# Decoder layer on one core: looks placed between the exponentials of the first attention, its norms moved ahead, and one of three context forms of each batch made in the own stage

## The chip, the cores and the metric
The kernel runs on one core of a Trainium2 chip. The metric is device time in microseconds (us) of one execution, from the first to the last instruction of the program with what lies around it; less is better. Before the change the median of three runs is 1250.8 us (1247.96 to 1253.37).

The core has five engines that run side by side, each through its own queue in order: PE (TensorE, the matmuls; PEld are its weight loads), DVE (VectorE), ACT (ScalarE), POOL (GpSimd) and SP (SyncE, which issues the DMAs). [...]

## What is computed
One decoder layer over x of 8 batches x 112 tokens x 512, in float32, with a context of 8 x 375 x 512:

```python
x = x + attn(layernorm(x))            # 16 heads of 32, rotary, causal, softmax
x = x + xattn(layernorm(x), context)  # see below
x = x + ffn(layernorm(x))             # ternary weights, silu(gate) * up, rms_norm, projection
```

The second line holds two attentions beside each other. The normed x is divided by an input scale, clipped and rounded to an 8-bit float. From it come q, k and v of the *own* attention (16 query heads and 8 key heads of 128, over the batch's own 112 tokens) and the query of the *context* attention, whose keys and values are projections of the context in full precision. Queries and keys are layer-normed per head. Both outputs are divided by a smoothing vector, rounded to 8 bits again, and go through one projection.

## The kernel before, in words
The order of the work is written out by hand: every engine runs its instructions in the order in which the Python code issues them. There is no planner that moves them. The work falls into four parts.

**First attention** (L417 to L745, about 0 to 168 us). The batches are treated in two halves of four (HB = 4).
- `norm_stats` and `ln_apply` norm a batch on DVE, with two small POOL steps between; `transposed(half)` turns the four normed batches on PE, and ACT copies them into hT.
- `project_qk(half, oc)` makes one of eight 128-row blocks of q and k for four batches: eight matmuls (L494), a bias copy qb on ACT (L502), a shuffle and a product on DVE (L506, L514), a product and a sum on POOL (L513, L515). qb and sw have two buffers each.
- `batch(b, last)` is software-pipelined over batches: `values(b)`, `attended(b - 2)`, `scores(b)`, `turned(b - 1)`, `softmaxed(b)`. In the first half `softmaxed` adds the mask and takes maxima on DVE (L570, L575), subtracts on POOL (L577) and takes exponentials on ACT (L580), for four banks r. `turned` transposes p on PE (L589) and copies it on ACT (L593). `attended` multiplies by v (L605), and DVE divides (L615, L616) into o, which has two buffers.
- `joined(b, ...)` adds o of batch b to x on POOL (L682), takes the statistics of batch b - 1 and norms batch b - 2 into h.
- `quantise_turn` transposes h (L347), `quantise_begin` scales it and takes magnitudes on ACT (L365, L215), and `quantise(n, ...)` clips on DVE (L219, L220) and finishes on POOL (L222, L391). They prepare the 8-bit input of the next part.
- `look(n)` reads through the projection weights of the cross attention once, in 32 pieces: each look is one ACT pass (L462) over a 128 x 512 piece of wp with a sum, to learn whether any low half of a weight is other than zero. A wp tile of 1 MB holds four looks, there are two buffers, and the fourth look of a tile issues the load of the tile after next. Thirteen looks stand among the first projections, four behind each of the first four batches, three among the second projections.

**Own stages** (units 0 to 31: four stages s of eight batches b, about 168 to 440 us). Each unit projects q, k and v of four heads, norms, scores, weighs and attends, with its later steps delayed by one to five units (`advance`). At the end of each unit stand the splitting of weights for later (`own_background`) and `form_parts`.

**Context stages** (units 32 to 63, four stages of eight batches, about 440 to 1057 us). A context batch is used in three pieces j of 125 positions, each in three float32 *forms* (rounded, mixed, rest; 750 KB in all). A form is made from 250 KB of raw context by an ACT copy, a POOL subtraction and a DVE mix, and stored to HBM by SP; later stages load it (`load_ct`). `keys(j)` multiplies piece j by the weights (L1013), ACT and DVE join the two banks (L1023, L1024), DVE takes statistics. Before the change `form_parts` makes the three forms of batch 0 in the own stage (begun in units 10, 14 and 18; the mix in the next unit, L1173; the store in the unit after that), and in the first context stage (s = 4) each unit b from 0 to 6 makes all three forms of batch b + 1 beside its own work with `make_begin` (ACT L1411, POOL L1412) and `make_end` (DVE L1418, store L1422). The tiles come from a pool of four. `made` and `ahead` (L261, L262) say which forms are made where; `queue` is the order in which SP loads raw weights and raw context through five buffers.

**Feed-forward** (about 1057 to 1249 us), with the ternary weights prepared earlier in pieces (`background`).

Of the kernel before, what the change touches and what calls it, by code (L numbers as in the profile page):

```python
# [20 lines left out]
B, S, H = 8, 112, 512  # L21
HB = B // 2
# [3 lines left out]
SC, NJ, CJ = 375, 3, 125  # L26
# [13 lines left out]
def decoder_layer(  # L40
# [39 lines left out]
    def uid(s):  # L80
        count[0] += 1
        return f"{s}_{count[0]}"
# [175 lines left out]
    queue = [(0, what, k) for what in (0, 1) for k in range(KC)]  # L258


    made = {b: [("form", b + 1, j) for j in range(NJ)] for b in range(B - 1)}  # L261
    ahead = [(0, j) for j in range(NJ)]  # L262
    for s in range(8):
        if s == 4:

# [110 lines left out]
    def quantise(n, begin=True):  # L376


        for _ in range(n):
            if begin:  # L380
                quantise_begin()
            t = qstate["clipped"]
            if t < qstate["begun"] - (2 if begin else 0):
                qstate["t", t] = round_a(*qstate.pop(("y", t)), s0, 4)
                qstate["clipped"] += 1
            t = qstate["done"]
            left = qstate["clipped"] - t
            if left > (1 if begin else 2) or (left and not begin and qstate["clipped"] == qstate["begun"]):
                _, half, k, m = qtiles[t]
                engine = nc.vector if half else nc.gpsimd  # L390
                engine.tensor_tensor(  # L391
                    xq[m][:, k, half * SH : (half + 1) * SH], *qstate.pop(("t", t)), ALU.subtract
                )
                qstate["done"] += 1
# [20 lines left out]
    with ExitStack() as st:  # L415
# [39 lines left out]
        def look(n):  # L455
            for _ in range(n):
                i, k = divmod(looks[0], KC)
                looks[0] += 1
                w = looked[i][:, k * 512 : (k + 1) * 512].bitcast(U16).rearrange("p (n two) -> p n two", two=2)
                half = w[:, :, 0:1].rearrange("p n o -> p (n o)")  # L460
                at = KC * i + k
                nc.scalar.activation(half, half, AF.Copy, accum_out=seen[:, at : at + 1])  # L462
                if k == KC - 1:
                    look_load()
# [97 lines left out]

        def softmaxed(banks, masked):

            ps_ = []
            for r in range(4):
                p = a2.tile([S, 4, S], F32, tag="p", name=uid("p"), bufs=8)
                s_ = banks[r][:S, :SH].rearrange("p (h t) -> p h t", t=S)
                if not masked:
                    nc.vector.tensor_tensor(  # L570
                        p, s_, mask.rearrange("p (o t) -> p o t", o=1).to_broadcast([S, 4, S]), ALU.add
                    )
                    s_ = p
                nm = sm("amx", 4)
                nc.vector.tensor_reduce(nm[:S], s_, AX.X, ALU.max, negate=True)  # L575
                engine = nc.vector if masked else nc.gpsimd
                engine.tensor_tensor(  # L577
                    p, s_, nm[:S].rearrange("p (h o) -> p h o", o=1).to_broadcast([S, 4, S]), ALU.add
                )
                nc.scalar.activation(p, p, AF.Exp)  # L580
                ps_.append(p)
            return ps_
# [82 lines left out]
        for i, oc in enumerate((0, 4, 1, 5, 2, 6, 3, 7)):  # L665
            project_qk(0, oc)
            if i > 2:
                look(2 if i < 5 else 3)
            if i == 1:
                for b in range(HB, B):  # L670
                    lns[b] = norm_stats(xb[b])
            elif i == 2:
                for b in range(HB, B):
                    ln_apply(b)
            elif i == 3:
                transposed(1)
        va, pr, pt = {}, {}, {}

        def joined(b, least, last):

            if b < last:
                nc.gpsimd.tensor_tensor(xb[b], xb[b], outs.pop(b), ALU.add)  # L682
            if least <= b - 1 < last:
                stats_x[b - 1] = norm_stats(xb[b - 1], True)
            if least <= b - 2 < last:
                h = s0.tile([S, H], F32, tag="h", name=uid("h"), bufs=4)
                norm_apply(h, xb[b - 2], *stats_x.pop(b - 2))
                normed_x[b - 2] = h
# [21 lines left out]

        for b in range(HB):
            batch(b, HB)
            look(4)
        for i, oc in enumerate((0, 4, 1, 5, 2, 6, 3, 7)):
            if i == HB + 3:
                quantise(3, False)
            project_qk(1, oc)
            if i < 3:
                look(1)
            if i < 2:  # L720
                batch(HB + i, HB)
            if i < HB + 2:
                joined(i, 0, HB)
            if i == HB + 2:
                for _ in range(3):
                    quantise_begin()
        first.close()
        for b in range(HB, B):
            batch(b, B, 3 if b < B - 1 else 0)
# [246 lines left out]
    class Context(Unit):  # L976
# [10 lines left out]
        def project(self, g):  # L987
            tile_ = self.b < NT
            if not self.makes:
                load_ct(g + 1, 0)  # L990
            if tile_:
                xqx = xqxs.pop(g)
                project_q(self, lambda k: xqx[:, k, :])
            advance("normed", g)
            advance("weigh", g)
            if tile_:
                qn = self.qn = Heads("cq", P, 4)
                qn.stats(*[self.pq[:, j * P : (j + 1) * P] for j in range(4)])
                qn.powers([(4, epsc[:, 3:4])])
            kn = self.kn = Heads("ckv", CJ, 6)  # L1000
            self.kv = []
            rounds = self.s == 4 and self.b + 2 < NT
            if rounds:
                round_q3(self.b + 2, 0)
            if self.makes:
                make_begin(g + 1, 0)

            def keys(j):
                ct, banks = cts.pop((g, j)), [pa(), pa()]
                for m, bank in ((0, 0), (1, 1), (2, 1)):  # L1010
                    for k in range(KC):
                        at = (m * KC + k) * CJ
                        nc.tensor.matmul(  # L1013
                            banks[bank][:CJ, :],
                            lhsT=ct[:, at : at + CJ] if ct.dtype == F32R else ct[:, at : at + CJ].bitcast(F32R),
                            rhs=split[self.s, 1, k][m],
                            start=(k == 0 and m == bank),
                            stop=(k == KC - 1 and m != 1),
                        )
                if j < NJ - 1 and not self.makes:  # L1020
                    load_ct(g + 1, j + 1)
                kv = c2.tile([CJ, 512], F32, tag="kv", name=uid("kv"), bufs=8)
                nc.scalar.activation(kv, banks[0][:CJ, :], AF.Copy, scale=1.0 - E12)  # L1023
                nc.vector.tensor_tensor(kv, kv, banks[1][:CJ, :], ALU.add)  # L1024
                self.kv.append(kv)
                kn.stats(*[kv[:, i * P : (i + 1) * P] for i in range(2)])

            keys(0)
            if self.makes:
                make_end(g + 1, 0)  # L1030
                make_begin(g + 1, 1)
            advance("out", g)
            background(2 * g)
            advance("turn_p", g)
            if rounds:
                round_q3(self.b + 2, 1)
            keys(1)
            if self.makes:
                make_end(g + 1, 1)
                make_begin(g + 1, 2)  # L1040
            if tile_:
                self.q = c2.tile([P, 512], F32, tag="q", name=uid("q"))
                for j in range(4):
                    qn.normalise(self.q[:, j * P : (j + 1) * P], self.pq[:, j * P : (j + 1) * P], j)
            background(2 * g + 1)
            context_splits(self.s, self.b)
            advance("attend", g)
            advance("turn", g)
            advance("rounded", g)
            split_end()  # L1050
            if rounds:
                round_q3(self.b + 2, 2)
            keys(2)
            if self.makes:
                make_end(g + 1, 2)
            if self.b == NT:
                drop(self.s, 1)
                if self.s < 7:
                    split_chunk(self.s + 1, 0, KC - 1)
            expand_q(g + 1)  # L1060
            kn.powers([(6, LN_EPS)])
            advance("score", g)
# [117 lines left out]
        nc.sync.dma_start(out=forms[b][:, j, :], in_=f.rearrange("p f c -> p (f c)").bitcast(F32))  # L1180


    fparts = {B + 2 + 4 * i: [i] for i in range(len(ahead))}

    def form_parts(i):

# [516 lines left out]
```

## Time and profile before

| | |
|---|---|
| Median of three runs | 1250.8 us |
| Profiled execution, its own time | 1251.02 us |
| Its span, first to last instruction | 1249.2 us |
| Mean granted clock of PE | 0.967 |
| PE, DVE, ACT, POOL busy | 94%, 72%, 67%, 64% of the span |
| Data moved by DMA | 151.37 MB, mean 121 GB/s |

The profile tells of one execution. A busy PE is not PE at its peak, since the ends of pipelined matmuls are modelled; so a stretch is judged by PE's idle time, by who ended it, and by the granted clock, which falls to half at times. Lines of the timeline give the start and the duration in us, the engine, the line of the kernel, the operation, what it writes and reads, its shape and how many follow each other; in brackets stands how long the engine had been idle and whose work ended that. A line of the view by stretches gives the stretch, its length, the busy time of PE, PEld, DVE, ACT and POOL with the number of instructions, the granted clock, the DMA engines' busy share and GB/s.

### The profile page before, as it was taken

How to read it: one execution, taken by the hardware profiler on the slowest of the kernel's cores; microseconds unless marked ns; L12 is line 12 of the kernel's file. 1: busy time of each engine (PE TensorE's matmuls, PEld its weight loads, DVE VectorE, ACT ScalarE, POOL GpSimd, SP SyncE). 2: the span in 40 equal slices, each digit the busy share in tenths (PEclk: the TensorE clock that was granted, in tenths of full speed). 3: DMA queues.
4: the chain of work that ended last, by engine and by line, in shares of the span. 5: the costliest groups of instructions: out<-in, count | busy, mean ns of one | idle time of the engine just before them, and what ended most of it. 6: DMA issues, size and time to landing. Idle time of an engine off the chain costs nothing. (4 is left out here: it accounts for less than half of the span.)

```text
span 1249.2 us, 19832 instructions
## 1 busy us (share of the span) xinstructions
PE 1178.3 (94%) x6312; PEld 932.0 (75%) x6312; DVE 903.2 (72%) x2365; ACT 843.1 (67%) x2083; POOL 805.3 (64%) x962
## 2 busy tenths in 40 slices
PE   8998987899999889999999999999999999999998
PEld 5474776787878767777777777787777877788886
DVE  6557877778887767786777768677776767577764
ACT  2752765978787856767667776677677676466643
POOL 5638746676767756876566676577574666476554
PEclk9988966999999998999999999999999999999999
DMA  7320130222221255456655455554554541122311
GB/s 243 135 68 0 53 118 1 75 87 83 69 85 40 74 178 170 160 179 219 191 160 173 153 176 171 178 162 159 185 159 149 183 155 36 43 90 68 106 51 60
DMA packets 55370, 151.37 MB, mean 121 GB/s; under 512 B 6384, under 2 KB 15728, under 8 KB 54240
## 3 DMA queue, kind: packets, MB, share of 16 engines
q1 hardware_dynamic: 55264, 150.07, 36.9%
q8 instruction: 52, 0.85, 0.3%
q14 instruction: 54, 0.44, 0.1%
HBM read 121.65 MB, written 26.56 MB: 119 GB/s over the span
## 5 line engine op out<-in xcount | busy, mean ns | idle before, releaser
L1013 PE MATMUL pa<-wx,ct 128*125 128x512 f32 x1152 | 294.9, 405 | 0.0
L1013 PEld LDWEIGHTS pa<-wx,ct 128*125 128x125 f32 x1152 | 213.3, 190 | 49.8
L222 POOL TENSOR_TENSOR f8t<-y,big 128x512 f32<-128x512 bf16 (+1 forms) x80 | 98.2, 1230 | 134.6 <-DVE big L220 134.5
L827 POOL TENSOR_TENSOR p<-p,ri 112x500 f32<-112x500 f32 (+1 forms) x128 | 128.5, 1025 | 36.5 <-DVE ri L822 35.2
L1024 DVE TENSOR_TENSOR kv<-kv,pa 125x512 f32<-125x512 f32 x96 | 65.8, 686 | 90.7 <-PE pa L1013 42.0
L1105 ACT ACTIVATE p<-ps,cmx 112x375 f32<-112x375 f32 x128 | 71.7, 573 | 83.6 <-DVE cmx L1104 83.6
L765 PE MATMUL pa<-hi,xq 128*128 128x512 f32 (+2 forms) x352 | 114.9, 351 | 1.6 <-DVE xq L391 1.1
L765 PE MATMUL pa<-lo,xq 128*128 128x512 f32 (+2 forms) x352 | 110.0, 337 | 0.9 <-DVE lo L326 0.9
L1381 PE MATMUL pa<-h3T,wf 128*128 128x512 f32 (+1 forms) x512 | 107.3, 368 | 0.5 <-ACT h3T L1354 0.2
L1381 PEld LDWEIGHTS pa<-h3T,wf 128*128 128x128 f32 x512 | 92.7, 188 | 12.3 <-DVE h3T L1355 1.0
L186 DVE BATCH_NORM_AGGREGATE mv<-bst 128x2 f32<-128x6 f32 (+1 forms) x472 | 86.0, 182 | 16.4
L816 ACT ACTIVATE qT<-ps,hln 128x448 f32<-128x448 f32 (+6 forms) x112 | 57.3, 565 | 47.0 <-PE ps L811 46.7
L1096 PE MATMUL ps<-kT,qT 128*112 128x375 f32 x256 | 86.2, 479 | 0.5 <-ACT kT L1082 0.5
L1272 POOL TENSOR_TENSOR th<-th,tw 128x512 bf16<-128x512 bf16 x48 | 57.3, 1194 | 45.2 <-DVE th L1264 33.4
L185 DVE BATCH_NORM_STATS2 bst<-pa 128x6 f32<-128x128 f32 x280 | 76.1, 272 | 13.9 <-PE pa L765 13.6
L205 ACT ACTIVATE kv<-kv,ckvnm,ckvr 125x128 f32<-125x128 f32 x192 | 77.4, 491 | 5.9 <-POOL ckvnm L201 5.8
L785 PE MATMUL ps<-hi,cq 128*128 128x512 f32 x224 | 78.7, 433 | 0.9 <-ACT p L1105 0.6
L1129 PE MATMUL ps<-pT,kv 125*128 125x224 f32 x384 | 78.0, 353 | 0.0
L765 PEld LDWEIGHTS pa<-hi,xq 128*128 128x128 f32 (+1 forms) x352 | 69.8, 198 | 6.9 <-DVE xq L391 1.8
L765 PEld LDWEIGHTS pa<-lo,xq 128*128 128x128 f32 (+1 forms) x352 | 70.0, 199 | 6.6 <-DVE lo L326 2.2
L1129 PEld LDWEIGHTS ps<-pT,kv 125*128 125x128 f32 x384 | 72.7, 190 | 1.9 <-ACT pT L1122 0.2
L847 POOL TENSOR_TENSOR cq<-f8t,big 128x512 fp32r<-128x512 f32 x56 | 66.0, 1179 | 4.4
(201 smaller groups left out, 3013.4 us busy)
## 6 DMA issues: line engine op xcount, KB each, us to landing
ct<-forms SPq DMA_DIRECT2D x75, 750.0 KB, 4.4
w<-in_wattn SPq DMA_DIRECT2D x96, 256.0 KB, 3.3
forms<-ct SPq DMA_DIRECT2D x21, 750.0 KB, 3.8
wp<-in_wattn SPq DMA_DIRECT2D x8, 1024.0 KB, 4.8
tr<-in_wgu SPq DMA_DIRECT2D x32, 256.0 KB, 4.5
done<-th SPq DMA_DIRECT2D x48, 128.0 KB, 4.3
wh<-done SPq DMA_DIRECT2D x24, 256.0 KB, 3.7
w<-in_ctxT SPq DMA_DIRECT2D x21, 250.0 KB, 3.5
```

Of the source, the lines that this page charges most:

```text
L185: nc.vector.bn_stats(st[: self.rows], a)
L186: nc.vector.bn_aggr(self.mv[: self.rows, self.at, :], st[: self.rows])
L205: nc.scalar.activation(dst, src, AF.Identity, bias=self.nm[:rows, i : i + 1], scale=self.r[:rows, i : i + 1])
L222: nc.gpsimd.tensor_tensor(t, y16, big, ALU.add)
L765: nc.tensor.matmul(out_, lhsT=lhsT, rhs=part[:, cut], start=first and i == 0, stop=last and i == 1)
L785: nc.tensor.matmul(po, lhsT=u.cq[:, j * P : (j + 1) * P], rhs=split[u.s, 2, j][i], **kw)
L827: nc.gpsimd.tensor_tensor(p, p, bc, ALU.mult)
L1013: nc.tensor.matmul(banks[bank][:CJ, :], lhsT=ct[:, at : at + CJ] if ct.dtype == F32R else ct[:, at : at + CJ].bitcast(F32R), rhs=split[sel ...
L1096: nc.tensor.matmul(pp[:S, :SC], lhsT=qT[:, j, :], rhs=self.kT[:, j // 2, :], start=True, stop=True,)
L1105: nc.scalar.activation(self.p[:, j, :], pp[:S, :SC], AF.Exp, bias=nm[:S], accum_out=self.sums[:S, j : j + 1])
L1129: nc.tensor.matmul(po[:, cut], lhsT=self.kv[j][:, 256 + g * P : 256 + (g + 1) * P], rhs=self.pT[:, j, cut], start=(j == 0), stop=(j == NJ ...
L1381: nc.tensor.matmul(pp[:, :n], lhsT=wcur[k][:, m * 256 + blk * P : m * 256 + (blk + 1) * P], rhs=hT[half, k][i], start=(k == 0 and i == 0), ...
```

## The change
- In the first half's `softmaxed` one look stands ahead of each of the four exponentials. The four looks behind each batch are gone, and the three among the second projections stand at i = 2, 3 and 4 instead of 0, 1 and 2. There are 32 looks as before.
- The statistics and norms of batches 4 to 7 stand behind the first and second projection instead of the second and third.
- `joined` of batches 0 and 1 stands behind batches 2 and 3 of the first half, and that of the next four behind the first four of the second projections. The first three `quantise_begin` stand one projection earlier (i = 5 instead of 6), and `quantise(3, False)` stands behind the last projection instead of ahead of it.
- Of each batch from 1 to 7 the third form (j = 2) is made in the own stage. `ahead` has ten forms instead of three, begun in every second unit from 10 to 28. In the first context stage a unit makes two forms and loads the third with `load_ct` after `keys(1)`; the queue of raw loads has seven entries fewer.

```diff
-    made = {b: [("form", b + 1, j) for j in range(NJ)] for b in range(B - 1)}
-    ahead = [(0, j) for j in range(NJ)]
+    made = {b: [("form", b + 1, j) for j in range(NJ - 1)] for b in range(B - 1)}
+    ahead = [(0, j) for j in range(NJ)] + [(b, NJ - 1) for b in range(1, B)]
...
+                if not masked:
+                    look(1)
                 nc.scalar.activation(p, p, AF.Exp)
...
             project_qk(0, oc)
             if i > 2:
                 look(2 if i < 5 else 3)
-            if i == 1:
+            if i == 0:
                 for b in range(HB, B):
                     lns[b] = norm_stats(xb[b])
-            elif i == 2:
+            elif i == 1:
                 for b in range(HB, B):
                     ln_apply(b)
...
         for b in range(HB):
             batch(b, HB)
-            look(4)
+            if b >= 2:
+                joined(b - 2, 0, HB)
         for i, oc in enumerate((0, 4, 1, 5, 2, 6, 3, 7)):
-            if i == HB + 3:
-                quantise(3, False)
             project_qk(1, oc)
-            if i < 3:
-                look(1)
             if i < 2:
                 batch(HB + i, HB)
-            if i < HB + 2:
-                joined(i, 0, HB)
-            if i == HB + 2:
+            if 2 <= i < 5:
+                look(1)
+            if i < HB:
+                joined(i + 2, 0, HB)
+            if i == HB + 1:
                 for _ in range(3):
                     quantise_begin()
+        quantise(3, False)
...
-                if j < NJ - 1 and not self.makes:
+                if j < NJ - 1 and not (self.makes and j < NJ - 2):
                     load_ct(g + 1, j + 1)
...
             keys(1)
             if self.makes:
                 make_end(g + 1, 1)
-                make_begin(g + 1, 2)
...
             keys(2)
-            if self.makes:
-                make_end(g + 1, 2)
...
-    fparts = {B + 2 + 4 * i: [i] for i in range(len(ahead))}
+    fparts = {B + 2 + 2 * i: [i] for i in range(len(ahead))}
```

## The prediction
> **What bounds the kernel now.** The first view is the page's busy shares: TensorE is busy 94% of a span of 1249.2 us, the next engine 72%. The chain that ended last names only the last matmuls (7%), so it does not say which earlier stretch decides. So I cut the span into stages by their first matmuls and asked for busy time by stage. Three rows (stretch, its length, then busy us of PE, PEld, DVE, ACT, POOL; granted clock; DMA share; GB/s):
> ```profile
> 83.75:126.04 42.29, 36.52 (x148) 20.52 (x147) 25.75 (x51) 13.38 (x27) 33.12 (x33) 0.85 0.00 1
> ...
> 440.50:601.80 161.30, 150.97 (x706) 116.84 (x704) 120.92 (x308) 108.55 (x259) 109.46 (x124) 0.96 0.53 178
> 601.80:754.20 152.40, 150.18 (x743) 118.00 (x743) 111.36 (x311) 110.52 (x262) 101.03 (x126) 1.00 0.53 169
> ```
> Row 1 is the second run of first-attention projections: PE stands still for 5.8 of 42.3 us, at a clock of 0.85. Rows 2 and 3 are the first context stage, which makes its forms, and the second, which loads them: 161.3 against 152.4 us, so making them costs at most 8.9 us. In the row of the own stage (252.4 to 375.6, not copied here) PE is busy 116.0 of 123.2 us, DVE and ACT 84%, the clock is 1.00 and the DMA share 0.24.
>
> Then the timeline of PE alone, for its waits in the first attention (start, us, operation; in brackets the idle time ahead and who ended it):
> ```profile
> 26.39 1.59 PE L481 MATMUL ps<-ident,h 112*128 112x112 f32 x12 [1.05 <-DVE h L173]
> 29.18 0.60 PE L481 MATMUL ps<-ident,h 112*128 112x112 f32 x4 [1.20 <-DVE h L173]
> ...
> 56.41 3.69 PE L521 MATMUL ps<-w,hT 128*112 128x512 f32 x8 [2.66 <-ACT pt L593]
> ...
> 111.07 0.32 PE L347 MATMUL ps<-ident,h 112*128 112x112 f32 x1 [1.25 <-DVE h L173]
> 114.61 0.45 PE L347 MATMUL ps<-ident,h 112*128 112x112 f32 x1 [3.22 <-DVE h L173]
> 114.85 5.83 PE L494 MATMUL pa<-hT,w 128*128 128x448 f32 x8
> ```
> The reader is to see that each wait is on a norm (h) or on a copy of ACT (pt), and that the last projection takes 5.83 us where the others take 3.05 (40 matmuls in 15.28 us from 94.35). A further wait of 1.31 on pt stands at 85.54, and the clock in the stretch from 113.4 to 120.1 is 0.50.
>
> **Part 1, first attention: -12.0 us.**
> (a) The norms of batches 4 to 7 start one projection, 3.0 us, earlier. Their inputs are there: the last xb lands at 18.67 us, and the statistics would start at 18.3. Then h is ready near 25 us, when PE gets to the transposes: -2.25 us (1.05 + 1.20). POOL does the same eight small steps one projection earlier; it is later caught by PE's pace of 3.0 us against its 2.75 (1.57 + 1.14 and a gap).
> (b) Looks. After the last exponential of a batch ACT runs four looks before it copies the turned p:
> ```profile
> 52.53 0.58 ACT L580 ACTIVATE p<-p 112x448 f32<-112x448 f32 x1 [0.61 <-POOL p L577]
> 53.02 0.76 ACT L462 ACTIVATE wp<-wp 128x512 uint16<-128x512 uint16 x1
> ...
> 55.85 1.81 ACT L593 COPY pt<-ps 112x448 f32<-112x448 f32 x4
> ```
> The looks take 2.8 us, and PE waits 2.66 of them at 56.41. Put between exponentials, a look and an exponential go every 0.72 + 0.50 = 1.22 us, and POOL's subtractions release one every 1.19 to 1.25 us, so they lie in ACT's 0.61 us gaps. Behind a look in ACT's queue stand an exponential and the copies: if a look's weights land late, PE waits again. A load takes 4.7 to 5.1 us and is issued some 7 us before its first use (four looks with their exponentials, 4.9, and four copies, 1.8), so I cost that at nothing. At batches 2 and 3 PE is already the bound (9.3 us a batch), so there ACT's gain is worth nothing. At 85.54 DVE's o also waited (3.34 us) for POOL's add into xb, which now comes two batches earlier; of the 1.31 us I take 0.5, since the turn needs two banks that o frees. Together -3.2.
> (c) joined runs two batches ahead, so POOL has two adds (1.26 to 1.65 us each) and one 0.74 us pair fewer among the projections, and h of batch 3 comes in the fourth projection; it was the seventh. My times: PE ends the sixth projection near 99 us, h is ready near 95. Both waits go: -4.5. The eight matmuls behind them ran at a granted clock of 0.50 and go back to 3.05 us: -2.8. The three quantise_begin are 4.4 us of ACT and now delay the qb of the seventh projection by 1.3 us; their clips and the four POOL steps (4.1 us) move behind the last projection. POOL's last qk comes 5.0 us after PE's last projection in both (125.5 - 120.5; 111.5 - 106.5). I add 0.7 for clips that stand in DVE ahead of batch 4's maxima. From 126 to 168 us PE is busy 41.45 of 41.96, and POOL was idle 5.8 at its start, so the moved work has room.
> Sum -2.25 - 3.2 - 4.5 - 2.8 + 0.7 = -12.0. Bounds: -7 if the clock does not come back and (b) is half lost; -15 if the 0.50 stretches at 72 and 82 us go too.
> The Trainium skill (TensorE: Matmul & The Clock Gate, "What's actually happening") says that the clock halves after an idle window of about 3.4 us. The trace agrees at 113, behind 3.22 us of waiting; but it shows a second case, where PE is busy throughout and the clock halves all the same:
> ```profile
> 59.00:72.30 13.30, 13.30 (x125) 10.50 (x124) 7.93 (x16) 8.73 (x21) 3.80 (x5) 1.00 0.27 93
> 72.40:75.70 3.30, 3.30 (x41) 3.10 (x42) 2.05 (x5) 2.05 (x7) 0.01 (x1) 0.50 0.41 107
> ```
> The same page ("Part 4: PE-mode transpose") has transposes not counting as busy, by which the 2.8 us of (c) need not come back (rival 1).
>
> **Part 2, seven more forms in the own stage: +5.5 us.** Each adds ACT 0.60, POOL 1.25 to 1.56, DVE 0.67 to 1.41 us, a load of 250 KB and a store of 750 KB (SP issues both; DMA is at 0.24, so nothing). They go into units 12, 16 and every second one from 20 to 28. What one costs is read from the three that are there, by the same matmul one unit apart, here with a mix between (unit 11):
> ```profile
> 274.69 0.28 PE L765 MATMUL pa<-hi,xq 128*112 128x256 f32 x1
> ...
> 283.00 0.28 PE L765 MATMUL pa<-hi,xq 128*112 128x256 f32 x1
> ```
> That is 8.31 us; the same place two stages on, units 26 to 27 without a form, goes from 399.15 to 406.76, 7.61 us: 0.7. The third form shows 0.7, the second 0.6. Queued behind the mix on DVE are the statistics of the next unit, for which POOL, ACT and then PE's transposes wait. 7 x 0.65 = 4.6, and 1 more because units 17, 25 and 29 also carry round_q3 or double splits. Bounds: 0, and all three engines in series by their means, 7 x (0.60 + 1.46 + 1.17) = 22.6.
> The Trainium skill (SBUF — State Buffer, "Who interferes with whom") says that a DVE step with two SBUF inputs and a GpSimd step that reads SBUF exclude each other for the whole step. The form's mix in this trace (0.67 or 1.41 us) agrees; this rule is rival 2.
>
> **Part 3, one form fewer per unit in the first context stage: -5 us.** The third mix stands on DVE right ahead of the score's maxima:
> ```profile
> 480.77 1.35 DVE L1418 SCALAR_TENSOR_TENSOR ct<-ct 128x500 fp32r<-128x500 f32 x1
> 482.05 1.90 DVE L1104 TENSOR_REDUCE cmx<-ps 112x1 f32<-112x375 f32 x4
> ```
> Without it maxima, exponentials, weighing and turn come 1.28 us sooner. PE waits for the weighing 1.03 us near 487, 1.25 near 528 and 2.4 near 588; the other units show no more than 0.3, their form is hidden already. I take 0.7 + 0.9 + 0.8 = 2.4. After the first two the clock falls to 0.5 and twelve matmuls take 4.5 us instead of 3.0: 3.0 if both go. Together -5.4, say -5. The 3.79 us wait at 467.72 hangs on POOL's cq, and stays. The load that replaces the form (4.4 us to land, issued 15 us ahead) waits only for PE's keys(1). Bounds: -1 and -8.9.
>
> **Sum**, against the profiled execution's 1251.0 us (its span 1249.2 and 1.8 around it; the median is 1250.8): 1251.0 - 12.0 + 5.5 - 5.0 = **1239.5 us**.
>
> **The rivals.** 1: the clock stays low behind the transposes and the context forms were hidden: 1251.0 - 9.2 + 5.5 - 1 = 1246.3. For it: the 0.50 at 72 us with PE busy. Against: the row at 113 has real waits. 2: each POOL subtraction holds a DVE step for its 1.46 us: + 10.2, so 1244.2; against it, three forms at 0.65. 3, **slower**: the own stage's loop takes each form in series, 3.2 us, and each gap brings a stretch at 0.5, 1.5 us more by the twelve matmuls above: 7 x 4.7 = 32.9, so 1251.0 - 17 + 32.9 = 1266.9. It decides from (12 + 5) / 7 = 2.4 us a form. For it: DVE and ACT are at 84%, and there are 10 forms in 22 units. Against: the clock was 1.00 with three forms there. 4: all of the stage's 8.9 us and 15 in the attention: 1251.0 - 15 + 4.6 - 8.9 = 1231.7. In the built order each look stands right ahead of an exponential and the adds ahead of the projections, so the change does what it says.
>
> **How the numbers follow.** Forecast 1233 to 1245: 0.60. Rival 1 (1244 to 1250): 0.15. Rival 2 (1242 to 1247): 0.10. Rival 3: 0.06. Rival 4 (1228 to 1233): 0.09. From 1231 to 1248 leaves out about 0.15. What can be told from no change is about 0.5%, 6.3 us: below 1244.5 lie 0.57 of the forecast, 0.09, half of rival 2 and a little of 1: 0.74; slower by it 0.06; the rest 0.20.
>
> **What would show it.** Right: no PE wait on h at L481 or L347 and none on pt near 52 us; batch 4's first maximum near 114 us, not 126; own units with a mix 0.6 to 0.8 us longer; the first context stage near 156 us. Wrong: ACT waiting for wp between exponentials, PE waits on q, k or p growing in the own stage, new stretches at half clock there, or a 42 us stretch before the own stage that has become longer.

## The result and the profile after

The changed kernel takes 1237.62 us (median of four runs, 1235.65 to 1239.85), the kernel before 1252.09 us (median of four runs, 1247.96 to 1253.42): a ratio of 0.9891, with a 95% interval of 0.9859 to 0.9922. A second measurement (experiment 12) gives 1238.08 us and 0.9890 (0.9869 to 0.9910). The forecast was 1239.5 us. The profiled execution takes 1238.58 us, its span is 1236.8 us, and the mean granted clock is 0.974 (before: 1251.02, 1249.2 and 0.967).

By stages, the kernel after. Columns as before: the stretch, its length, busy us of PE, PEld, DVE, ACT and POOL, granted clock, DMA share, GB/s. The first row runs from the turning of batch 3's p, 1.2 us earlier in the work than the row of before, to batch 4's first maximum; the second is the first context stage, the third the second:
```profile
76.06:112.39 36.33, 35.78 (x163) 20.98 (x163) 24.60 (x49) 14.35 (x27) 28.87 (x27) 0.95 0.04 13
434.90:587.40 152.50, 145.47 (x706) 113.81 (x704) 112.61 (x301) 105.13 (x252) 97.06 (x117) 0.98 0.54 188
587.40:739.70 152.30, 150.04 (x742) 117.95 (x742) 111.34 (x311) 110.25 (x262) 100.81 (x126) 1.00 0.52 169
```
The reader is to see two things. Around the second run of projections PE stands still for 0.6 us, where the row of before lost 5.8. And the first context stage, which still makes two forms a unit, now takes no longer than the second, which loads them all: 152.5 against 152.3 us. It was 161.3, so 8.8 of the 8.9 us that the prediction took as a bound are gained, not 5.

The timeline of PE after the change, at the places where before had waits on norms and on ACT's copies:
```profile
23.78 0.60 PE L481 MATMUL ps<-ident,h 112*128 112x112 f32 x4 [0.85 <-DVE h L173]
25.05 1.06 PE L481 MATMUL ps<-ident,h 112*128 112x112 f32 x8 [0.67 <-DVE h L173]
...
49.93 1.53 PE L521 MATMUL ps<-w,hT 128*112 128x512 f32 x3
...
97.59 0.55 PE L347 MATMUL ps<-ident,h 112*128 112x112 f32 x4
97.97 3.56 PE L494 MATMUL pa<-hT,w 128*128 128x448 f32 x9
```
The wait of 2.66 us on pt is gone (L521 at 49.93 has no bracket), so are both waits on h at L347, and the last projections follow without a gap. At L481 0.85 and 0.67 us of the 1.05 and 1.20 are left in this profile.

To see where the time went I take the same matmuls as markers in several profiles and compare the times between them (us). The first five columns lead from the first projection to the fifth, to the second run of projections, to its third, to its eighth, and to the first own unit. "Own stages" is from the first unit of the second own stage to the first context unit; the first own stage, left out here, takes 75.8 to 76.3 us in all of them. The kernels are those of the experiments below.

| kernel | to 5th | to 2nd run | to its 3rd | to its 8th | to 1st own unit | own stages | first context stage |
|---|---|---|---|---|---|---|---|
| before | 17.8 | 46.8 | 17.9 | 20.5 | 61.4 | 192.3 | 159.4 |
| forms alone | 16.6 | 48.5 | 17.9 | 20.5 | 61.4 | 199.6 | 150.6 |
| looks alone | 16.6 | 42.4 | 15.7 | 20.5 | 58.2 | 192.2 | 158.2 |
| joined alone | 16.8 | 49.1 | 17.0 | 15.5 | 60.1 | 192.0 | 160.9 |
| attention alone | 13.7 | 42.6 | 15.6 | 15.5 | 60.1 | 192.2 | 158.3 |
| after | 15.7 | 44.0 | 15.5 | 15.5 | 60.0 | 202.2 | 150.6 |
| after, again | 14.6 | 43.9 | 15.8 | 15.5 | 60.1 | 202.3 | 150.6 |
| other units | 14.9 | 45.6 | 15.5 | 15.5 | 63.1 | 196.4 | 149.8 |

The remaining stages differ little (152.2 to 152.3 us for the second context stage, 152.4 to 152.7 for the third, 336.6 to 339.0 from there to the end of the last matmul). So the profile after against that of before: about 15 us less in the first attention (1.5 of them because its first projection starts earlier, at 10.3 instead of 11.8 us), 9.9 more in the own stages, 8.8 less in the first context stage, 2 more behind it, where a half-clock stretch of 3.4 us stands at 1066.

### The profile page after: what moved, and what is told of

It reads as the page before. It is cut to its first block, busy times and chain, and to the rows that moved or that the text cites. A ratio compares the mean times of both kernels' runs of the same rounds, so it can differ in the third digit from the quotient of the medians.

```text
span 1236.8 us, 19851 instructions
## 1 busy us (share of the span) xinstructions
PE 1169.5 (95%) x6312; PEld 927.0 (75%) x6312; DVE 905.8 (73%) x2365; ACT 840.6 (68%) x2083; POOL 798.2 (65%) x962
## 5 line engine op out<-in xcount | busy, mean ns | idle before, releaser
L1016 PE MATMUL pa<-wx,ct 128*125 128x512 f32 x1152 | 291.0, 401 | 0.0
L1016 PEld LDWEIGHTS pa<-wx,ct 128*125 128x125 f32 x1152 | 210.3, 187 | 48.8 <-issue 0.2
```

Of the source, the lines that this page charges most:

```text
L1016: nc.tensor.matmul(banks[bank][:CJ, :], lhsT=ct[:, at : at + CJ] if ct.dtype == F32R else ct[:, at : at + CJ].bitcast(F32R), rhs=split[sel ...
```

## The experiments

Diffs are against the kernel after unless the text says before.

**1. The attention part alone.**
The kernel after with the forms made as before; against the kernel after:
```diff
-    made = {b: [("form", b + 1, j) for j in range(NJ - 1)] for b in range(B - 1)}
-    ahead = [(0, j) for j in range(NJ)] + [(b, NJ - 1) for b in range(1, B)]
+    made = {b: [("form", b + 1, j) for j in range(NJ)] for b in range(B - 1)}
+    ahead = [(0, j) for j in range(NJ)]
...
```


> The kernel before with the first-attention part of the change alone; all three forms of a batch are made as before. The theory read from the two traces (the own stage begins 15.5 us earlier after the change, and 1.5 of it is an earlier start of the first projections that has nothing to do with the edit): 13 to 15.5 us less than before, that is 1237 to 1239 us, with the first own unit's marker near 161 us instead of 176.3. The prediction's sum: 12 us less, 1240. Rival: the clock takes the gain back later in the span, and less than 10 us are left, 1242 or more.

Measured: 1235.49 us against 1249.79, ratio 0.9878 (0.9844 to 0.9913), 14.3 us less. The own stages and the first context stage are as before (192.2 and 158.3 us); nothing is taken back later.

**2. The forms part alone.**
The kernel before with the rest of the change, that is with these lines and those of load_ct, make_begin, make_end and fparts:
```diff
-    ahead = [(0, j) for j in range(NJ)]
+    ahead = [(0, j) for j in range(NJ)] + [(b, NJ - 1) for b in range(1, B)]
...
```


> The kernel before with the forms part of the change alone. The theory from the traces: the own stage 9.9 us longer, the first context stage 8.8 us shorter, in all 1 us more than before, 1253. The prediction's terms: 5.5 more and 5.0 less, in all 0.5 more. The times cannot tell these apart, the two stretches of the trace can: 202 us against 198 from the second own unit to the first context unit, and 150.6 against 154.4 for the first context stage. Rival: the 9.9 us belong to another phase of the clock that the earlier start brought, and here the own stage grows by no more than 6.

Measured: 1252.28 us against 1249.79, ratio 1.001 (0.999 to 1.003). The two stretches: 199.6 us (7.3 more than before) and 150.6 (8.8 less). Both terms were predicted too small, and they cancel: by itself this part wins nothing, so the whole change is worth what its attention part is worth. The own stages lie between the theory and its rival. How the waits and the clock share the difference is seen in unit 17. PE's wait there is the same here as in the kernel after, 2.38 and 2.42 us, but the clock behind it is not. The wait in the kernel after and with the forms alone, and then the row of the stretch behind it in each:
```profile
310.85 0.44 PE L929 MATMUL ps<-ident,k 128*128 128x128 f32 x2 [2.42 <-DVE x L802]
```
```profile
326.62 0.44 PE L926 MATMUL ps<-ident,k 128*128 128x128 f32 x2 [2.38 <-DVE x L799]
```
```profile
312.00:315.40 3.40, 3.40 (x14) 2.87 (x13) 3.37 (x10) 3.19 (x9) 3.09 (x5) 0.50 0.01 2
```
```profile
327.80:331.20 3.40, 3.40 (x24) 2.53 (x23) 3.37 (x10) 3.19 (x9) 3.09 (x5) 1.00 0.00 2
```
With the clock at 0.50, 14 matmul records stand in 3.4 us where 24 do at 1.00. Unit 17 takes 11.9 us in the one and 10.3 in the other (9.3 before).

**3. The ten forms in other units.**
```diff
-    fparts = {B + 2 + 2 * i: [i] for i in range(len(ahead))}
+    fparts = {n: [i] for i, n in enumerate((10, 12, 14, 17, 18, 20, 22, 25, 26, 27))}
```


> The kernel after, with the ten forms begun in units 10, 12, 14, 17, 18, 20, 22, 25, 26 and 27, so that no mix stands in units 17, 25 and 29, where roundings of the cross attention's input or double splits are done. Theory: in those three units the mix lengthens a PE wait from about 1.1 to 2.4 us and a half-clock stretch follows, 2.6 us a form; elsewhere a form costs 0.7 or less. Then the own stage becomes 3 x (2.6 - 0.7) = 5.7 us shorter than after: about 1232 us where after has 1237.6, and the half-clock stretches near 312 and 377 us are gone. Rival: a form costs 1.4 us on average wherever it stands, since it is the engines' total load that counts; then no change against after, 1237 to 1239, or more because neighbouring units now carry forms.

Measured: 1230.42 us, ratio 0.983 (0.9801 to 0.9859), below the interval of the kernel after (0.9869 to 0.9910 in its second measurement). The own stages take 196.4 us, 5.8 less than after; units 17, 25 and 29 are back at 9.3, 9.3 and 10.1 us, and the half-clock stretches at 312 and 377 us are gone. Seven more forms now cost 4.2 us against the attention alone (192.2), 0.6 each on average. The rows of the own stages, attention alone, after and other units, one fence each:
```profile
234.34:426.54 192.20, 176.74 (x1204) 150.88 (x1203) 155.19 (x485) 158.35 (x493) 138.34 (x182) 0.99 0.23 75
```
```profile
236.90:439.10 202.20, 180.78 (x1204) 154.21 (x1203) 163.85 (x492) 160.76 (x500) 145.44 (x189) 0.97 0.31 107
```
```profile
240.65:437.05 196.40, 177.07 (x1204) 150.50 (x1203) 160.83 (x492) 160.70 (x500) 144.70 (x189) 0.99 0.33 111
```
Length less PE's busy time is PE's idle time: 15.5, 21.4 and 19.3 us. Of the 10 us that the forms cost after, 6 are idle time and 4 are the same 1204 matmuls at a lower clock (180.8 busy against 176.7). With the forms in other units 3.9 us of idle time are left and 0.3 of clock. The waits that grew are these, attention alone and then after (engine and line, whom PE waited for: total, times, longest):
```profile
PE ps L942 <- DVE kT L934: 5.1, 5, 1.6
PE ps L929 <- DVE x L802: 3.0, 3, 1.3
```
```profile
PE ps L942 <- DVE kT L934: 9.0, 7, 2.3
PE ps L929 <- DVE x L802: 5.6, 3, 2.4
```
Of the waits on x those of units 17 and 25 grew. Of the waits on kT the longest is that of unit 29; the others that grew stand in units 13, 14, 21 and 22, behind the forms begun in units 12 and 20. Those two forms stay in the other units' kernel and cost 1.4 us each there too, and the rest from 0 to 0.7: the 0.6 is an average, not a price.

**4. Three third forms instead of seven.**
```diff
-    made = {b: [("form", b + 1, j) for j in range(NJ - 1)] for b in range(B - 1)}
-    ahead = [(0, j) for j in range(NJ)] + [(b, NJ - 1) for b in range(1, B)]
+    moved = (1, 3, 5)
+    made = {b: [("form", b + 1, j) for j in range(NJ - (b + 1 in moved))] for b in range(B - 1)}
+    ahead = [(0, j) for j in range(NJ)] + [(b, NJ - 1) for b in moved]
...
```


> The kernel after, with the third form of batches 1, 3 and 5 alone made in the own stage (begun in units 18, 20 and 22, batch 0's in 10, 12 and 14); batches 2, 4, 6 and 7 have all three made in the first context stage as before. Theory: the gain of the context stage sits in single units whose PE waits and half-clock stretches go (1.3, 3.3 and 2.9 us in its units 0, 2 and 4, of 8.8), while the own stage pays 0.7 us for each of three forms: 1252 - 15 + 2 - 7.5 = 1231.5 us. Rival: the gain goes with the number of mixes that DVE is rid of, 3/7 of 8.8 = 3.8 us, which gives 1235.

Measured: 1235.91 us, ratio 0.9881 (0.9852 to 0.9909). The first context stage takes 154.3 us, 4.0 less than with the attention alone: the rival's 3/7, not the theory's 7.5. The own stages take 196.1, 3.9 more and not 2, since the forms begun in units 12 and 20 lengthen two units each (by 0.9 and 0.5 to 0.8). So the theory of gains in single units falls; the 4.0 us fit the rival, by which they go with the number of mixes that DVE is rid of.

**5 and 6. Which of a form's steps costs the time: the mix or the subtraction?** In the kernel after, DVE first, then POOL, around unit 17 and in unit 28 (start, us):
```profile
306.45 1.35 DVE L219 TENSOR_SCALAR y<-y 128x512 bf16<-128x512 bf16 x1
...
404.94 3.52 DVE L219 TENSOR_SCALAR y<-y 128x512 bf16<-128x512 bf16 x1 [2.13 <-ACT big L215]
```
```profile
306.04 1.60 POOL L1167 TENSOR_TENSOR form<-raw,form 128x500 fp32r<-128x500 f32 x1 [0.24 <-ACT k L205]
...
404.58 2.53 POOL L309 TENSOR_TENSOR w<-w,wx 128x512 f32<-128x512 f32 x2
407.08 1.23 POOL L1167 TENSOR_TENSOR form<-raw,form 128x500 fp32r<-128x500 f32 x1
```
The clip of L219 takes 0.29 us where POOL is idle (302.62 us with the attention alone). Here it ends 0.1 to 0.2 us after a POOL step: 1.35 us beside the form's subtraction, and 3.52 beside three POOL steps in a row, two of a weight split and the form's. Two kernels tell mix and subtraction apart:
```diff
+        if i in (3, 7, 9):
+            nc.scalar.copy(f[:, 1, :], f[:, 0, :].bitcast(F32))
+            return
         nc.vector.scalar_tensor_tensor(
```


> The kernel after; in units 17, 25 and 29 the DVE mix of the form is left out and a copy on ACT (about 0.6 us) fills its place, so that three forms lack their mixed part. The prediction's theory (the mix is queued on DVE ahead of the next unit's statistics) lets these units fall back by what the form cost them, 2.4 to 2.7 us each in the profile after. The theory now: the PE wait of 2.42 us at 310.85 stands ahead of that unit's mix, and comes from the POOL subtraction at 306.04 (1.60 us), beside which DVE's clip takes 1.35 instead of 0.29 us, and 3.52 in unit 28. Then units 17 and 25 stay 1 us and more above the 9.3 and 8.9 us that they take without a form, and unit 29 stays at 12.5.

```diff
-        nc.gpsimd.tensor_tensor(f[:, 2, :], w, f[:, 0, :].bitcast(F32), ALU.subtract)
+        nc.scalar.copy(f[:, 2, :], w)
```


> The kernel after; all ten forms made in the own stage get their rest from a copy on ACT (about 0.6 us) and not from the POOL subtraction, so these forms are wrong; the mixes stay. Theory: units 17, 25 and 29 go back to 9.3, 9.3 and 10.1 us, the clips there to 0.3 us, and the own stage (second own unit to first context unit) from 202.2 to 196 us or less; the whole near 1231. Rival (the mix is the price, and ACT is now 6 us busier): these units stay above 10 us, the own stage at 200 us or more, the whole at 1237 or more.

Measured, without the three mixes: PE's waits in units 17, 25 and 29 are 2.41, 2.42 and 2.26 us, as after (2.42, 2.42, 2.25). The units take 11.8, 10.4 and 11.3 us, the last two without the half clock that after has behind these waits. The time is that of one run, 1235.19 us. Without the ten subtractions: the units take 9.3, 9.3 and 10.1 us, the own stages 194.7 us. The time is 1235.22 us, ratio 0.9873 (0.9844 to 0.9901); the 4 us more than I expected lie outside the own stages (the first own unit starts at 163.0 us, the first context stage takes 151.5). The same two steps of unit 17, without the mix and then without the subtraction:
```profile
306.96 1.35 DVE L219 TENSOR_SCALAR y<-y 128x512 bf16<-128x512 bf16 x1
...
311.36 0.44 PE L929 MATMUL ps<-ident,k 128*128 128x128 f32 x2 [2.41 <-DVE x L802]
```
```profile
307.74 0.28 DVE L219 TENSOR_SCALAR y<-y 128x512 bf16<-128x512 bf16 x1
...
311.07 0.44 PE L929 MATMUL ps<-ident,k 128*128 128x128 f32 x2 [1.33 <-DVE x L802]
```
So it is the subtraction: it holds up a DVE step for 1.07 us, and PE's wait is 1.08 us longer. The mix adds nothing to PE's waits in these three units. It was not taken out of units 13, 14, 21 and 22; without the subtraction units 13 and 14 take 8.0 and 6.6 us (after 8.5 and 7.1, attention alone 7.6 and 6.6), so there too the subtraction is the larger part. The Trainium skill (SBUF — State Buffer, "Who interferes with whom") says that a DVE step in a two-port mode and a GpSimd step lock each other out for a whole instruction. The trace agrees with 1.35 us against 0.28, if the clip runs in such a mode, which no view names; and it shows that DVE is not let in between POOL steps that follow each other closely, at 404.94.

**7. The looks alone**, against the kernel before.
```diff
+                if not masked:
+                    look(1)
                 nc.scalar.activation(p, p, AF.Exp)
...
             batch(b, HB)
-            look(4)
```


> The kernel before with the looks alone moved: one ahead of each exponential of the first half and none behind the batches; norms, joined, quantise and forms as before. Theory: the looks are worth more than the 3.2 us that the prediction gave them, because the half-clock stretches between 72 and 89 us go with the waits on pt; from the fifth first projection to the second run of projections 47 us become 43 to 45, and from there to the third of the second run 17.9 become 15.6: 5 to 6 us in all, 1244 to 1246. Rival: PE's waits between 77 and 94 us hang on DVE's o, which waits for POOL's add of joined, so the second stretch stays at 17.9 and 3 us are won, 1247 to 1248.

Measured: 1238.86 us against 1252.21, ratio 0.9892 (0.9871 to 0.9913), 13.4 us less. That is more than the theory's 6 and nearly what the whole attention part wins. From the fifth projection to the second run, before and then the looks alone:
```profile
29.61:76.45 46.84, 43.81 (x306) 27.89 (x305) 27.29 (x54) 31.90 (x77) 26.19 (x28) 0.96 0.37 127
```
```profile
27.06:69.46 42.40, 42.03 (x306) 26.37 (x305) 26.55 (x53) 30.96 (x77) 25.42 (x27) 1.00 0.44 150
```
PE's idle time falls from 3.0 to 0.4 us, as predicted (2.66), and its busy time by 1.8 as the granted clock goes from 0.96 to 1.00. To the third projection it is 15.7 us instead of 17.9. These two stretches give 6.7 us against before, and 7.7 against the mean of the three kernels with the old looks (48.2 and 17.6). The rest in this profile lies where the edit changes nothing: 1.3 at the start, 1.3 in the first projections, 3.2 from the last one to the first own unit (5.7 us at half clock behind batch 6's values instead of 15.1) and 1.1 in the first context stage.

**8. Joined, quantise_begin and clips alone**, against the kernel before.
```diff
+            if b >= 2:
+                joined(b - 2, 0, HB)
...
-            if i == HB + 3:
-                quantise(3, False)
...
-            if i < HB + 2:
-                joined(i, 0, HB)
-            if i == HB + 2:
+            if i < HB:
+                joined(i + 2, 0, HB)
+            if i == HB + 1:
                 for _ in range(3):
                     quantise_begin()
+        quantise(3, False)
```


> The kernel before with joined two batches ahead, the quantise_begin one projection earlier and the clips behind the last projection, and nothing else of the change. Theory: the waits of 1.25 and 3.22 us on h and the half clock behind them go; from the third projection of the second run to the end of the eighth 26.2 us become 18.5, and 1 us is given back before the own stage: 6 to 7 us, 1243 to 1245. Rival: with the looks still behind the batches, ACT or PE is late elsewhere and the waits on h only move, less than 3 us, 1248 or more.

Measured: 1249.03 us, ratio 0.9975 (0.9959 to 0.9991), 3.2 us less. From the third to the eighth projection 15.5 us instead of 20.5, and batch 4's values follow 3.0 us behind the start of the eighth, with the old order (looks alone) 5.4: 7.4 us won, as predicted (4.5 and 2.8). But then more is lost than the 1 us of the theory. From batch 4's values to batch 6's it is 13.8 us before and with the forms alone and 14.0 with the looks alone, all with the old order, and 18.3 here and 18.2 with the whole attention part. So 4.3 us are given back, 2.2 of them idle time of PE and 2.1 busy time, with 3.4 us at half clock where the old order has none. The time agrees: 7.4 less 4.3 is 3.1. The place in the kernel after, first DVE, then POOL, then PE:
```profile
106.17 1.21 DVE L219 TENSOR_SCALAR y<-y 128x448 bf16<-128x448 bf16 x1
107.30 1.22 DVE L220 TENSOR_SCALAR big<-big 128x448 bf16<-128x448 bf16 x1
108.44 0.26 DVE L219 TENSOR_SCALAR y<-y 128x448 bf16<-128x448 bf16 x1
108.62 1.20 DVE L220 TENSOR_SCALAR big<-big 128x448 bf16<-128x448 bf16 x1
109.75 1.10 DVE L219 TENSOR_SCALAR y<-y 128x448 bf16<-128x448 bf16 x1
110.77 1.10 DVE L220 TENSOR_SCALAR big<-big 128x448 bf16<-128x448 bf16 x1
```
```profile
105.70 1.54 POOL L515 TENSOR_TENSOR qk<-qb,sw 128x448 f32<-128x448 f32 x1
107.21 1.18 POOL L513 TENSOR_TENSOR qb<-qb,tab 128x448 f32<-128x448 f32 x1
108.46 1.23 POOL L515 TENSOR_TENSOR qk<-qb,sw 128x448 f32<-128x448 f32 x1
109.65 2.08 POOL L222 TENSOR_TENSOR f8t<-y,big 128x448 f32<-128x448 bf16 x2
```
```profile
115.00 0.43 PE L544 MATMUL pa<-maskr,identr 112*112 112x448 f32 x1 [0.62 <-DVE p L578]
116.18 0.42 PE L544 MATMUL pa<-maskr,identr 112*112 112x448 f32 x1 [0.76 <-DVE p L578]
117.37 0.66 PE L544 MATMUL pa<-maskr,identr 112*112 112x448 f32 x1 [0.77 <-DVE p L578]
```
Five of the six clips last until about 0.1 us after a POOL step ends; the one of 0.26 us slips into a gap of POOL. Six steps of 0.26 us would be 1.6 us; these are 6.1, and batch 4's maxima stand behind them. PE waits 0.62, 0.76 and 0.77 us for these, and a half-clock stretch follows at 117.4.

**9. The clips back ahead of the last projection.**
```diff
+            if i == HB + 3:
+                quantise(3, False)
             project_qk(1, oc)
...
-        quantise(3, False)
         first.close()
```


> The kernel after with the three clips ahead of the last projection of the first attention, where they were before the change (the quantise_begin stay one projection early). The theory for the part of the first attention's gain that is lost again (from 16.5 us at values of batch 4 to 12.1 us at values of batch 6): six clips take 1.1 to 1.2 us each beside POOL and stand ahead of batch 4's maxima, so PE waits 0.6 to 0.8 us three times at 115 to 117 us and the clock halves behind it. With the clips earlier these three waits go, 2 to 4 us of the 1237.6. Rival: they now delay the last q and k, as they stand on DVE ahead of its shuffle and product, and nothing is won, 1237 to 1239.

Measured: 1240.71 us, ratio 0.9918 (0.9891 to 0.9944), no better than after; the 3 us more lie within the intervals. The rival had the reason, but not the size:
```profile
113.98 0.73 PE L554 MATMUL pa<-qk,qk 32*112 32x112 f32 x8 [4.96 <-POOL qk L515]
```
Ahead of the last projection the slowed clips delay DVE's shuffle and product, and with them POOL's last qk; PE waits 4.96 us for it, where after has 0.55 us here and 2.15 in the three waits above. Neither place lets the clips run undisturbed.

**10. Odd units, and 11. cheap units.**
```diff
+    fparts = {n: [i] for i, n in enumerate((10, 11, 13, 15, 17, 19, 21, 23, 25, 27))}
```


> The kernel after with the ten forms begun in units 10, 11, 13, 15, 17, 19, 21, 23, 25 and 27, so that the subtraction runs beside another unit's clips each time. Theory: what a form costs is set by which DVE step its POOL subtraction meets and by whether POOL has other two-input steps queued right ahead of it, not by the number of forms: units that now carry a begin after weight splits on POOL lose 2 us and more, others nothing; between 1228 and 1236 us. Theory of an even price (0.6 us each, as in the run with other units): 1230 to 1232. It also tells what unit 19 costs without a mix: 8.3 us if the weight split in it is what makes it longer than unit 27, 7.6 if the form was, as the prediction read it.

```diff
+    fparts = {n: [i] for i, n in enumerate((10, 11, 14, 17, 18, 19, 22, 25, 26, 27))}
```


> The kernel after with the ten forms begun in the units that cost least in the runs with other units: 10, 11, 14, 17, 18, 19, 22, 25, 26 and 27. Theory (the price of a form is set by the DVE steps that its subtraction meets, so it goes by the unit): 0.4 us for 11, 0.7 for 17 and 19, 0.5 for 22, 0.6 for 25 to 27, so the own stage takes 194.5 us against 196.5 in the two runs with other units and 202.2 after; about 1228 us. Rival (an even 0.6 us a form): 196.5 us in the stretch and 1230 in all.

Measured: odd units 1230.05 us, ratio 0.9844 (0.9817 to 0.9871), own stages 196.5 us; cheap units 1234.31 us, ratio 0.9844 (0.9822 to 0.9867), own stages 194.5 us. The price by unit holds for the stretch of the cheap units (194.5 expected), but the 2 us are lost in the spread of the first attention. The odd units fit both of their theories and decide nothing: PE's idle time in their own stages is the least of the three sets (17.0 us against 17.8 and 19.3), but 10.2 us of that stretch are at half clock instead of 3.4. The times tell all three sets of units from the kernel after, by about 0.5% (the interval of the odd units just touches that of the second measurement of after, 0.9871 and 0.9869), not from each other. Unit 19 takes 7.9 us with a form begun in it and no mix, 8.3 with a mix, and 9.0 with a mix where a form was also begun in unit 17 (other and cheap units); unit 27 takes 7.6 with or without a mix. So of the 0.7 us that the prediction read as the price of a form, about 0.3 were a difference between the two units; by the code, unit 27 lacks a weight split that units 11 and 19 have.

**12. The kernel after once more.**

> The kernel after, unchanged, on the same chip as the others of this call, so that the moved forms can be compared with it: 1237 us. The own stage again takes 200 to 202 us with units 17 and 25 above 10 us and unit 29 above 11; where these stand by a chance of the clock's grid, they move by 1.5 us, where by the subtraction, the three PE waits are 2.2 to 2.5 us again. The first own unit starts anywhere from 158 to 165 us, as it did in the seven profiles with the same first attention.

Measured: 1238.08 us; own stages 202.3 us, units 17, 25 and 29 at 11.8, 11.6 and 12.4 us, first own unit at 160.4.

## Why the prediction was right, and where it was not

The forecast of 1239.5 us is 1.9 us off, but four of its terms are off by 3.5 to 4.5 us each: looks and context won more, clips and own stages cost more. That the sum is close is luck. Two signs of being wrong came all the same: PE's waits on x and kT grew in the own stage, and new half-clock stretches stand there at 312 and 377 us.

- **(a) Norms, -2.25.** From the first to the fifth projection 13.7 us in the attention alone, 14.6 to 15.7 in the kernel after, 16.6 to 17.8 without the edit: 2.9 between the best of each. PE stands idle there for 2.3 us in all four profiles without the edit and for 0.0 to 1.5 with it. The mechanism holds, and the size where no wait is left; in the profile after two thirds of the wait stayed. The norms were not tried alone.
- **(b) Looks, -3.2.** Mis-sized: 6.7 to 7.7 us in the two stretches, 13.4 in the time. The wait of 2.66 us went as told, and in the two stretches PE's idle time falls from 4.3 to 0.5 us, about the 3.2 that I counted; the busy time falls by 2.9 besides. The step that failed is the clock: I counted half-clock stretches only behind the waits on h, and kept those at 72 and 82 us for the bound of -15. With the looks alone one stretch of 3.4 us is left there instead of 10.2. That profile met the clock well, but the gain does not hang on it: the eleven profiles with the looks moved take 58.0 to 61.6 us for the two stretches together, with 3.4 to 10.2 us at half clock, the three without 64.7 to 66.4, with 10.2 to 13.7.
- **(c) joined, -6.6.** The 4.5 and 2.8 us went, also with the projections' clock at 1.00 again, so rival 1 is out. (Before the change the clock fell at 113.3, 1.3 us before the wait of 3.22 us was over, not behind it.) The failed term is the 0.7 for the clips, which measured 4.3. It was too small for six undisturbed clips, and these stand beside POOL's steps: rival 2 had this exclusion of DVE and POOL, and I did not apply it here. Alone, (c) is worth 3.2 us.
- **Part 1, -12.0.** Measured 14.3, and near 15 by the first own unit (176.3 and 176.4 us in the two profiles with the old attention; 158.3 to 165.7, mean 161, in nine with the new one); from the start of the first projection it is 14.
- **Part 2, +5.5.** Measured 9.9, and 7.3 in the run whose clock did not fall in units 17 and 25. The base of 0.65 a form holds as an average in the other units (0.6), though the pair of units it was read from was not alike and the price goes from 0 to 1.4 by the unit. What failed is the 1 us for units 17, 25 and 29, which take 7.7 us more than with the attention alone, and the mechanism there: not the mix that is queued ahead of the statistics, but the POOL subtraction of the unit before, which holds DVE's clip. Rival 2 had that mechanism, with 1.46 us for each of seven forms; it decides in three of them, and the clock can more than double it there.
- **Part 3, -5.** Measured 8.8, the bound. The mechanism holds; the wait at 467.72 stayed (3.3 us). PE's waits in the first context stage, before and after (engine and line, total, times, longest):
```profile
PE ps L1117 <- POOL p L827: 3.8, 10, 0.8
PE ps L962 <- POOL p L827: 3.8, 1, 3.8
```
```profile
PE ps L965 <- POOL p L830: 3.3, 1, 3.3
PE ps L1117 <- POOL p L830: 0.9, 3, 0.3
```
  The waits for the weighing fall by 2.9 us (I took 2.4; of the 2.4 near 588, 1.34 was a wait on ACT's pT, which stays). All of PE's idle time there falls by 3.3 (161.3 - 151.0 against 152.5 - 145.5), and the rest, 5.5 us, is busy time (I took 3.0). The time at half clock falls from 13.7 us to 6.8, 1.6 of them with PE idle, which accounts for about 4 of the 5.5; the remainder is open.

Rival 3 did not happen: the forms in the own stages cost 1.4 us each, below the 2.4 at which the change would have lost. Rival 4's attention and context came true together, and were paid for by the own stages.

**Open.** With the looks alone the time is 6 to 7 us better than their two stretches say, and norms and joined together add 2 us to it by the ratios (0.9878 against 0.9892), but 6 by the markers (2.9 and 3.1); the intervals of the two ratios are too wide to tell 2 from 6. About 3 of the unexplained us stand between batch 6's values and the first own unit: 41.9 us in both profiles of the old first attention, with 15.1 us at half clock, and 38.8 with the looks alone, with joined alone and with the attention alone, with 5.7 to 5.9. Either edit seems to win them, so that the two gains would not add. But other profiles with the new order take up to 42.1 us there, so how much is the clock's place in single runs was not settled.

## What to carry to other kernels

Before a POOL step is put into a loop, look which short DVE step will run beside it: a 0.28 us clip took 3.52 us here, until three POOL steps queued back to back had ended. Choose the unit by that, not by the engines' mean load; moving three of ten forms won 5.8 us in the own stages. And price a removed wait with the half-clock stretch behind it: in this kernel the clock gave about as much as the waits themselves (looks: 3.8 us of idle and 2.9 of busy time; first context stage: 3.3 and 5.5).

## What the runs showed of the hardware

In the traces' clock records every half-clock stretch inside the program lasts 3.41 us or a multiple of it, on a grid that lies elsewhere in each execution, and the same code meets it differently. The stretch from the fifth projection to the second run, in the kernels with other units and with three forms moved, has the same instructions:
```profile
25.15:70.74 45.59, 45.22 (x307) 29.39 (x305) 29.92 (x57) 32.70 (x81) 29.16 (x30) 0.93 0.43 147
```
```profile
24.44:66.94 42.50, 42.03 (x307) 26.39 (x305) 28.86 (x56) 32.88 (x82) 28.80 (x30) 1.00 0.46 160
```
PE is busy all but 0.4 and 0.5 us in both, and yet the clock falls twice in the first and not in the second: 3.1 us. (Many of these matmuls are transposes; whether they count as busy for the clock, which rival 1 denies, no run separates.) Over the whole first attention the nine profiles differ by 7.4 us, so a stage must be compared in several profiles before 3 us are put down to an edit. The Trainium skill (TensorE: Matmul & The Clock Gate, "What's actually happening") has a free-running window of 3413 ns; the steps of 3.41 us agree. That section ties the low clock to idle windows, and here it comes with PE busy by the profile, and behind a wait of 2.42 us in one execution but not behind 2.38 in another.
